# A four-layer graph attention stack on Trainium2: layer 0 with SyncE in program order, x loaded four targets at a time, input copies between the first gathers, and the target bias added by VectorE

## The chip, the core and the metric

The program runs on one core of one Trainium2 chip. The metric is the device time of one execution in microseconds, the median of several runs. The engines are called here as the profile calls them: PE (TensorE), DVE (VectorE), ACT (ScalarE), POOL (GpSimd) and SP (SyncE). SP computes nothing and only issues transfers (DMAs). Transfers are issued from three engines: SP and ACT[...], and POOL[...].[...]

## What is computed

There are 3327 nodes with 256 features, and a symmetric adjacency matrix in which about one entry in a hundred is set, so that a node has some 33 neighbours. Four layers follow each other; each is `x = layernorm(x + attention(x))`. The change touches layer 0 only:

```
g_src = x @ W_src_w.T + W_src_b                      # [n, 256]
g_tgt = x @ W_tgt_w.T + W_tgt_b                      # [n, 256]
score[i, j] = sum_c leaky_relu(g_src[i] + g_tgt[j], 0.2)[c] * a_w[c]
weights = softmax over j of score, only where adj[i, j] != 0
x = layernorm(x + weights @ g_tgt)
```

Because the weights of a row sum to one, `weights @ g_tgt` equals `weights @ (x @ W_tgt_w.T) + W_tgt_b`. The kernel uses this: the table of targets holds the rows without their bias, the bias is put into the source term for the scores, and it is added once to the output.

## The kernel before

Layers 1 to 3 treat the adjacency as dense and are mostly matmuls. Layer 0 (`sparse0`, L269) is sparse: for each node it makes a list of its neighbours, gathers their rows from a table in DRAM, and works on nothing else. The 26 tiles of 128 nodes are split into four sets of 4, 7, 9 and 6 tiles (`SETS`). Within a set nodes are sorted by their number of neighbours, so that a tile needs as many gathers as its largest node: 56 in the first tile of a set, fewer in the later ones (`LEVELS`). Four gathers make a part; there are about 245 parts in all, counted by q.

The work runs in this order.

1. **Setup.** Constants, weights (`w_tgt`, `w_src`), the row `a_row`, the biases in a tile `bias`, and the transposed x in seven banks of 512 nodes (`columns_wide`, L323, issued by ACT at L330). The banks lie in buffers that the gathers use later. `load` (L303) brings pieces of the adjacency, 128 rows by 1024 columns of int32, into three buffers `adj_i`, by SP.
2. **Targets and the neighbour lists of set 0.** A loop over the 26 tiles makes the rows of targets on PE from the banks of x (`targets`), which ACT copies out and POOL stores into `table_d`. Between them run the steps of `neighbours(0)`: ACT converts a piece of the adjacency (`convert`, L524), PE turns it into column numbers (`fill`), and DVE finds the largest eight again and again (`scan` at L560, `sort`), which gives each node's list. `sources` makes the source rows and stores them to `own_d` from ACT. For tiles of later sets it loads its columns of x itself into `xt` (L428, SP, four buffers). At the end DVE ranks the nodes of a set (L659 to L663).
3. **Gathers and scores.** A loop over the parts q runs, at each step: some steps of the later sets' `neighbours`, whatever is due at this step, the gathers of part q + 8 (`LEAD`) on POOL (L756), and the scores of part q on DVE (L776 and L782). After a tile's last part, ACT scales the gathered rows (L829), PE adds them up (L832), DVE adds the input (`add_input`, L852) and POOL scatters the result back (`put_back`, L869). `write_list` (L712) stores the lists of a later set in sorted order, and `read_lists` (L720) reads them back.

Each set has an array `own_d` in DRAM with a row per node: the negated source term, the input row at column 257 (`AT_X`), and the node's own target row at column 513 (`AT_TGT`). `gather_own` (L744) fetches these rows in sorted order. They are put together from four sides: `sources` writes the first part, `keep_inputs` (L384) copies the input from x, DRAM to DRAM, `add_bias` (L389, the transfer at L392) adds `b_tgt` to the input in DRAM with an accumulating transfer on POOL, and a copy on SP brings the target rows from `table_d`.

Who orders the work: within `sparse0` a `manual_schedule` names PE, DVE, ACT and POOL, and these run their instructions in the order of the program. SP isn't named, so the planner of the framework may move its transfers ahead of where the program has them.[...] `at_step(q, ...)` puts a piece of work at step q of the third loop; `between` holds small POOL pieces that are put between two gathers.

In the program the copies for sets 1 to 3 stand after the second loop:

```
            for s in range(1, len(SETS)):
                lo, hi = starts[s] * P, min(n, (starts[s] + SETS[s]) * P)
                keep_inputs(s, nc.sync)
                copy_rows(nc.sync, own_d[s][: hi - lo, AT_TGT:], table_d[1 + lo : 1 + hi, :])
                at_step(4 + 2 * s, between.append, lambda s=s: add_bias(s))
```

In the trace, SP issues the copies of inputs at 9.01 to 26.5 us, the copies of target rows at 83.84, 104.47 and 117.47 us, and POOL the three bias transfers at 201.03, 231.90 and 260.44 us.

Of the kernel before, what the change touches and what calls it, by code (L numbers as in the profile page):

```python
# [8 lines left out]
F32 = mybir.dt.float32  # L9
# [5 lines left out]
ALU = mybir.AluOpType  # L15
# [4 lines left out]
P = 128  # L20
# [4 lines left out]
BIG = 1e30  # L25
# [7 lines left out]
SETS = (4, 7, 9, 6)  # L33
# [10 lines left out]
AT_X = 257  # L44
AT_TGT = 513
# [4 lines left out]
def gat_stack(  # L50
# [29 lines left out]
    nc = tc.nc  # L80
    n, dim = x.shape
# [24 lines left out]
    table_d = dram.tile([n + 1, ROW], F32, name="table_d")  # L106
# [13 lines left out]
    def copy_rows(engine, dst, src):  # L120

        rows = dst.shape[0]
        whole = rows // 16 * 16
        for lo, hi in ((0, whole), (whole, rows)):
            if lo < hi:
                engine.dma_start(dst[lo:hi], src[lo:hi])
# [93 lines left out]
    banks_n = [(lo, min(n, lo + BANK)) for lo in range(0, n, BANK)]  # L220
# [48 lines left out]
    def sparse0(lost):  # L269
        GROUP, TURNS, LEAD, SPREAD = 4, 22, 8, 8  # L270
        starts = [sum(SETS[:s]) for s in range(len(SETS))]
        with ExitStack() as s0:
# [5 lines left out]
                tc.manual_schedule(  # L278
                    engines={
                        mybir.EngineType.PE, mybir.EngineType.DVE, mybir.EngineType.Activation,  # L280
                        mybir.EngineType.Pool,
                    }
                )
            )
# [18 lines left out]
            def load(s, t, p):  # L303
                lo, hi = pieces[p]
                it, pn = starts[s] + t, rows_of(starts[s] + t)
                adj_i = loaded[s, t, p] = io0.tile(
                    [P, PIECE], I32, tag="adj_i", name="adj_i", bufs=3
                )
                copy_rows(nc.sync, adj_i[:pn, : hi - lo], adj[it * P : it * P + pn, lo:hi])

            for p in range(3):
                load(0, 0, p)

            w_tgt = const0.tile([P, kc, ROW], F32, name="w_tgt0")
            nc.scalar.dma_start(w_tgt[:, :, :dim], w_tgt_t.rearrange("(c p) f -> p c f", p=P))
            a_row = const0.tile([P, dim], F32, name="a_row")
# [6 lines left out]
            def columns_wide(b):  # L323
                lo, hi = banks_n[b]
                t = gath.tile(
                    [P, GROUP, ROW], F32, tag=f"g{(TURNS - 1 - b + SHIFT) % TURNS}", name="x_wide"
                )
                t = t.rearrange("p a b -> p (a b)")[:, : kc * BANK]
                t = wide_x[b] = t.rearrange("p (k i) -> p k i", k=kc)
                nc.scalar.dma_start(t[:, :, : hi - lo], x_t_p[:, :, lo:hi])  # L330

            columns_wide(0)
            w_src = const0.tile([P, kc, dim + 1], F32, name="w_src0")
            nc.scalar.dma_start(w_src[:, :, :dim], w_src_t.rearrange("(c p) f -> p c f", p=P))
            bias = const0.tile([1, 2, dim + 1], F32, name="bias0")
            bs_row = bias[:, 0, :]
            nc.scalar.dma_start(bias[:, 0, :dim], b_src[None])
            nc.scalar.dma_start(bias[:, 1, :dim], b_tgt[None])
            for b in range(1, len(banks_n)):
                columns_wide(b)  # L340

            raised = const0.tile([P, P], BF16, name="raised")
            nc.vector.tensor_scalar_mul(raised, ident, float(BASE))
            minus_one = const0.tile([P, P], BF16, name="minus_one")
# [39 lines left out]
            def keep_inputs(s, engine):  # L384

                lo, hi = starts[s] * P, min(n, (starts[s] + SETS[s]) * P)
                copy_rows(engine, own_d[s][: hi - lo, AT_X : AT_X + dim], x[lo:hi, :])

            def add_bias(s):  # L389

                lo, hi = starts[s] * P, min(n, (starts[s] + SETS[s]) * P)
                nc.gpsimd.dma_start(  # L392
                    own_d[s][: hi - lo, AT_X : AT_X + dim],
                    b_tgt[None].to_broadcast([hi - lo, dim]), accum_op=ALU.add,
                )

            keep_inputs(0, nc.gpsimd)
            add_bias(0)

            nc.vector.memset(w_tgt[:, :, dim:], 0.0)  # L400
            nc.vector.memset(w_src[:, :, dim:], 0.0)
            nc.vector.memset(bias[:, :, dim:], BIG)
# [4 lines left out]
            def score_columns():  # L407
                for c in range(kc):
                    t = io0.tile([P, dim], F32, tag="minus", name="dots0")
                    nc.vector.tensor_mul(t, w_tgt[:, c, :dim], a_row)  # L410
                    nc.vector.tensor_reduce(w_tgt[:, c, dim : dim + 1], t, axis=AX.X, op=ALU.add)
                nc.vector.tensor_scalar_mul(w_tgt[:, :, dim], w_tgt[:, :, dim], SLOPE)
                nc.vector.tensor_add(bs_row[:, :dim], bs_row[:, :dim], bias[:, 1, :dim])
                nc.scalar.mul(a_ps[:, :dim], a_row, 1.0 - SLOPE)
                nc.scalar.copy(a_ps[:, dim : dim + 1], ones[:, :1])

# [320 lines left out]
            between = []  # L737
# [114 lines left out]
            def add_input(s, t):  # L852

                entry = held[s, t]
                inv = io0.tile([P, 1], F32, tag="inv0", name="inv0")
                nc.vector.reciprocal(inv, entry["total"])
                y = entry["y"] = io0.tile([P, dim], F32, tag="hs", name="hs")
                nc.vector.scalar_tensor_tensor(
                    y, entry["acc"][:, 0, :], inv, entry["own"][:, AT_X : AT_X + dim],
                    op0=ALU.mult, op1=ALU.add,  # L860
                )
                nc.vector.scalar_tensor_tensor(
                    y, entry["acc"][:, 1, :], inv, y, op0=ALU.mult, op1=ALU.add
                )

            def put_back(s, t):

# [116 lines left out]
            nc.scalar.dma_start(table_d[0:1, :], none)  # L984


            first = neighbours(0)
# [29 lines left out]
            def at_step(q, what, *args):  # L1017
                due.setdefault(q, []).append(lambda: what(*args))
# [40 lines left out]


            ahead, owed, steps = [], {}, 0
            for s in range(1, len(SETS)):
# [827 lines left out]
```

## Time and profile before

| what | value |
|---|---|
| median of 3 runs | 3480.82 us (3480.5 to 3486.92) |
| the profiled execution | 3106.54 us |
| its span, first to last instruction | 3104.8 us |
| mean granted PE clock | 0.866 |
| PE busy | 2339.8 us (75%) |
| DVE busy | 2137.5 us (69%) |
| POOL busy | 1036.3 us (33%) |
| ACT busy | 869.1 us (28%) |
| gathers (L756), POOL | 945, of 949 ns each |
| first gather of layer 0 issued | 126.65 us |
| last scatter of layer 0 issued | 1487.07 us |

The profile describes one execution. Its times count from the first instruction. The page gives the busy time of each engine, the same in 40 equal slices, the groups of instructions that cost most, and what ended the idle time before each group. Other views give the instructions in order of time, the busy time within chosen stretches, and who waited for whom. In a line such as `POOL L756 DMA_INDIRECT g<-table_d,lst` the engine comes first, then the line of the kernel, the operation, and output and inputs by name. An issue of a transfer has a q behind its engine's name (`SPq`, `ACTq`), except on POOL. The time of an issue is not that of the data: the landing is told apart. A bracket at the end of a line holds the idle time before the instruction and what ended it. The DMA share is the mean busy share of the 16 engines.

### The profile page before, as it was taken

The page shows a single profiled execution, that of the slowest core. Times are in us where ns is not written, and L with a number is a line of the kernel's source. Part 1 is how long each engine was busy: PE and PEld are TensorE (multiplying, and loading weights), DVE is VectorE, ACT ScalarE, POOL GpSimd, SP SyncE. Part 2 cuts the span into 40 slices and gives each one's busy share as a digit, 9 for nine tenths or more (in the row PEclk, how much of TensorE's full clock was granted, in tenths as well). Part 3 has the DMA queues.
Part 4 walks back from the last instruction along what each step waited for, and adds up shares of the span by engine and source line. Part 5 has one row for each costly group of instructions (what it writes and reads, how often), then busy time and mean ns, then how long its engine had stood idle before and what let it go on. Part 6 is the DMA issues. An engine that isn't in the chain of part 4 may idle for free.

```text
span 3104.8 us, 45392 instructions
## 1 busy us (share of the span) xinstructions
PE 2339.8 (75%) x16046; PEld 1294.9 (42%) x16046; DVE 2137.5 (69%) x5575; ACT 869.1 (28%) x2426; POOL 1036.3 (33%) x1108
## 2 busy tenths in 40 slices
PE   3554666455454442736799999999999999999997
PEld 2322222222121211313688888884434545444342
DVE  3686988686787535755345532118898899899997
ACT  2233535343343331625234421110110110120110
POOL 1455777777777777776000000000000000000000
PEclk9657767777677776868899999999999999999998
DMA  8687676555654435644677643342212212212211
GB/s 207 195 187 139 171 186 172 141 138 147 146 141 114 114 103 109 147 112 110 207 237 210 196 137 93 102 116 62 66 46 71 68 47 70 66 46 61 56 47 48
DMA packets 183699, 374.90 MB, mean 121 GB/s; under 512 B 34847, under 2 KB 123375, under 8 KB 182440
## 3 DMA queue, kind: packets, MB, share of 16 engines
q0 software_dynamic: 56384, 164.24, 22.0%
q1 hardware_dynamic: 101946, 174.63, 20.2%
q10 hardware_dynamic: 25134, 33.04, 3.1%
q8 instruction: 130, 2.13, 0.3%
q14 instruction: 105, 0.86, 0.1%
HBM read 332.01 MB, written 49.53 MB: 123 GB/s over the span
## 4 chain that ended last, share of the span: by engine, by line
PE 46%; DVE 4%; DMA 1%; issue 1%; ACT 0%; SPq 0%; POOL 0%; POOLq 0%; DVEq 0%; ACTq 0%
PE acc L1545 18%; PE acc L1498 16%; PE acc L1553 9%; PE misc L1344 3%; DVE e L1414 2%; DMA at<-at_d 1%; DMA at_i<-in_adj_t_dram 1%; PE misc L1441 0%; PE misc L1627 0%; PE misc L1588 0%; DVE stats L1705 0%; DVE h L1703 0%; DVE both L1700 0%; DVE h L248 0%; DVE h L1518 0%
## 5 line engine op out<-in xcount | busy, mean ns | idle before, releaser
L756 POOL DMA_INDIRECT g<-table_d,lst x945 | 897.2, 949 | 333.1 <-issue 258.5
L1414 DVE SCALAR_TENSOR_TENSOR e<-rate,feat,at 128x896 f32<-128x896 f32 (+4 forms) x832 | 844.1, 1080 | 80.1 <-PE acc L1553 69.7
L832 PE MATMUL acc<-g,ident 128*128 128x512 f32 x958 | 526.5, 696 | 350.5 <-ACT g L829 321.7
L1545 PE MATMUL acc<-e,feat 128*32 128x384 f32 (+2 forms) x6656 | 688.4, 516 | 4.7 <-DVE e L1414 2.1
L776 DVE TENSOR_TENSOR y<-g,minus_ps 128x1028 f32<-128x1028 f32 (+2 forms) x245 | 289.1, 1180 | 251.8 <-DMA g<-table_d,lst 239.0
L832 PEld LDWEIGHTS acc<-g,ident 128*128 128x128 f32 x958 | 207.1, 225 | 591.8 <-ACT g L829 459.6
L1545 PEld LDWEIGHTS acc<-e,feat 128*32 128x32 f32 x6656 | 259.9, 110 | 342.0 <-issue 229.0
L829 ACT ACTIVATE g<-g,w 128x256 f32<-128x256 f32 x945 | 389.5, 494 | 8.8 <-issue 4.5
L1553 PE MATMUL acc<-e,feat 128*32 128x384 f32 (+3 forms) x3328 | 375.2, 513 | 0.0
L782 DVE SCALAR_TENSOR_TENSOR y<-y,a_ps 128x257 f32<-128x257 f32 x945 | 342.7, 418 | 7.5
L1498 PE MATMUL acc<-feat,e 128*128 128x257 f32 (+2 forms) x1352 | 305.0, 383 | 15.2 <-DMA l3aw<-in_l_w_dram 14.1
L1498 PEld LDWEIGHTS acc<-feat,e 128*128 128x128 f32 (+2 forms) x1352 | 256.3, 192 | 53.0 <-issue 15.1
L242 POOL TENSOR_TENSOR rstds<-rstds,minus_half 128x7 f32<-128x7 f32 (+1 forms) x12 | 19.7, 1644 | 773.0 <-DVE rstds L241 773.0
L534 PE MATMUL v<-code,leads 65*128 65x512 bf16 (+1 forms) x182 | 83.2, 459 | 232.9 <-DVE cand L560 183.5
L1498 PE MATMUL acc<-feat,at 128*128 128x257 bf16 (+2 forms) x2028 | 239.0, 275 | 8.3 <-DMA at<-at_d 8.1
L1498 PEld LDWEIGHTS <-at 128*128 128x128 bf16 (+2 forms) x2028 | 199.1, 99 | 42.9 <-DMA at<-at_d 6.5
L1553 PEld LDWEIGHTS acc<-e,feat 128*32 128x32 f32 (+1 forms) x3328 | 139.8, 110 | 155.4 <-issue 130.3
L560 DVE MAX8 cand<-v 128x8 f32<-128x104 f32 (+2 forms) x858 | 159.1, 260 | 15.5 <-PE v L537 15.5
L1414 DVE SCALAR_TENSOR_TENSOR e<-rate,feat,at_i 128x896 f32<-128x896 f32 (+2 forms) x104 | 111.6, 1081 | 78.9 <-DMA at_i<-in_adj_t_dram 61.2
L1394 POOL DMA_DIRECT2D rate3b_d<-rate_rows x4 | 2.1, 524 | 468.0 <-ACT rate_rows L1393 468.0
L534 PEld LDWEIGHTS <-leads 65*128 65x128 bf16 x182 | 20.4, 112 | 266.7 <-DVE cand L560 219.6
L1431 ACT CAST at<-at_i 128x896 bf16<-128x896 int32 (+2 forms) x104 | 92.0, 885 | 104.3 <-DMA at_i<-in_adj_t_dram 88.3
(205 smaller groups left out, 1776.0 us busy)
## 6 DMA issues: line engine op xcount, KB each, us to landing
adj_i<-in_adj_dram SPq DMA_DIRECT2D x75, 512.0 KB, 4.2
at<-at_d SPq DMA_DIRECT2D x150, 224.0 KB, 2.5
at_i<-in_adj_t_dram SPq DMA_DIRECT2D x50, 448.0 KB, 4.1
g<-table_d,lst POOLq DMA_INDIRECT x945, 2.9
at<-at_d SPq DMA_DIRECT2D x75, 192.0 KB, 2.4
at<-at_d SPq DMA_DIRECT2D x75, 191.8 KB, 2.3
at_d<-at ACTq DMA_DIRECT2D x50, 224.0 KB, 4.3
at_i<-in_adj_t_dram SPq DMA_DIRECT2D x25, 384.0 KB, 3.4
```

The source lines that it names most:

```text
L534: nc.tensor.matmul(v[:, :w], leads[:, b, :], code[:, :w], start=True, stop=False)
L560: nc.vector.max(spread[:, c0 + c, :], view(v[:, :w]))
L756: nc.gpsimd.indirect_dma_start(out=g[:, k - k0, :], out_offset=None, in_=table_d[:, :], in_offset=bass.IndirectOffsetOnAxis(ap=entry["lst" ...
L776: nc.vector.tensor_tensor(y, rows, minus_src[:, None, :].to_broadcast([P, m, dim + 1]), op=ALU.max)
L782: nc.vector.scalar_tensor_tensor(y, y, 1.0, a_ps[:, : dim + 1], op0=ALU.mult, op1=ALU.mult, accum_out=sc)
L829: nc.scalar.activation(rows, rows, AF.Copy, scale=w[:, k : k + 1])
L832: nc.tensor.matmul(dst, ident, rows, start=start, stop=stop)
L1344: nc.tensor.matmul(pacc[:pn, : dim + self.extra], ht[:, k, :pn], self.weight[:, k, :], start=(k == 0), stop=(k == kc - 1),)
L1414: nc.vector.scalar_tensor_tensor(e[:pn, : c1 - c0], self.rate[b][:pn, h_of, : c1 - c0], q, at[:pn, : c1 - c0], op0=ALU.max, op1=ALU.mult,)
L1498: nc.tensor.matmul(accs[s][:pn, : dim + 1], a[:pj, s * P : s * P + pn], f[:pj, : dim + 1], start=(j == 0 and part == 0), stop=(j == nt - 1 ...
L1545: nc.tensor.matmul(accs[x][p][q : q + 32, : hi - lo], f[:pj, at0 : at0 + 32], es[at0 // hd][:pj, lo:hi], start=(j == 0), stop=(j == nt - 1),)
L1553: nc.tensor.matmul(accs[x][pairs][h_of * 32 : (h_of + 1) * 32, : hi - lo], f[:pj, dim + h_of : dim + h_of + 1].to_broadcast([pj, 32]), es[ ...
```

## The change

SP is added to the engines that run in program order within `sparse0`. The banks of x are issued by SP instead of ACT: two before the loop, and the other five in the loop over targets, one every four tiles (at tiles 2, 6, 10, 14 and 18). The tile `bias` is split into a row `bs_row` and a tile `bt_rows`, which holds `b_tgt` in all 128 partitions. The accumulating transfers (`add_bias`) are gone; `add_input` adds `bt_rows` on DVE instead. `keep_inputs(0)` moves from the setup to tile 9 of the target loop. For the sets s = 1, 2, 3 the copy of inputs is put at step 5s of the third loop and the copy of target rows (`keep_targets`) at step 5s + 2; both stay on SP. The table's first row is stored by POOL instead of ACT.

```
-                        mybir.EngineType.Pool,
+                        mybir.EngineType.Pool, mybir.EngineType.SP,
...
-            for p in range(3):
-                load(0, 0, p)
...
-                nc.scalar.dma_start(t[:, :, : hi - lo], x_t_p[:, :, lo:hi])
-
+                nc.sync.dma_start(t[:, :, : hi - lo], x_t_p[:, :, lo:hi])
+
+            load(0, 0, 0)
             columns_wide(0)
+            load(0, 0, 1)
+            load(0, 0, 2)
+            columns_wide(1)
             w_src = const0.tile([P, kc, dim + 1], F32, name="w_src0")
             nc.scalar.dma_start(w_src[:, :, :dim], w_src_t.rearrange("(c p) f -> p c f", p=P))
-            bias = const0.tile([1, 2, dim + 1], F32, name="bias0")
-            bs_row = bias[:, 0, :]
-            nc.scalar.dma_start(bias[:, 0, :dim], b_src[None])
-            nc.scalar.dma_start(bias[:, 1, :dim], b_tgt[None])
-            for b in range(1, len(banks_n)):
-                columns_wide(b)
-
+            bt_rows = const0.tile([P, dim], F32, name="bt_rows")
+            bs_row = const0.tile([1, dim + 1], F32, name="bs_row")
+            nc.scalar.dma_start(bs_row[:, :dim], b_src[None])
+            nc.scalar.dma_start(
+                bt_rows, bass.AP(tensor=b_tgt.tensor, offset=b_tgt.offset, ap=[[0, P], [1, dim]])
+            )
...
-            def add_bias(s):
-
-                lo, hi = starts[s] * P, min(n, (starts[s] + SETS[s]) * P)
-                nc.gpsimd.dma_start(
-                    own_d[s][: hi - lo, AT_X : AT_X + dim],
-                    b_tgt[None].to_broadcast([hi - lo, dim]), accum_op=ALU.add,
-                )
-
-            keep_inputs(0, nc.gpsimd)
-            add_bias(0)
-
...
-                nc.vector.tensor_add(bs_row[:, :dim], bs_row[:, :dim], bias[:, 1, :dim])
+                nc.vector.tensor_add(bs_row[:, :dim], bs_row[:, :dim], bt_rows[:1, :])
...
+                nc.vector.tensor_add(y, y, bt_rows)
...
-            nc.scalar.dma_start(table_d[0:1, :], none)
+            nc.gpsimd.dma_start(table_d[0:1, :], none)
...
             for it in range(nt):
+                if it % 4 == 2 and it // 4 + 2 < len(banks_n):
+                    columns_wide(it // 4 + 2)
+                if it == 9:
+                    keep_inputs(0, nc.gpsimd)
                 row = targets(it)
...
+            def keep_targets(s):
+                lo, hi = starts[s] * P, min(n, (starts[s] + SETS[s]) * P)
+                copy_rows(nc.sync, own_d[s][: hi - lo, AT_TGT:], table_d[1 + lo : 1 + hi, :])
+
             for s in range(1, len(SETS)):
-                lo, hi = starts[s] * P, min(n, (starts[s] + SETS[s]) * P)
-                keep_inputs(s, nc.sync)
-                copy_rows(nc.sync, own_d[s][: hi - lo, AT_TGT:], table_d[1 + lo : 1 + hi, :])
-                at_step(4 + 2 * s, between.append, lambda s=s: add_bias(s))
-
+                at_step(5 * s, keep_inputs, s, nc.sync)
+                at_step(5 * s + 2, keep_targets, s)
```

More of the change, by code (lines that the diff above doesn't have):

```diff
@@ L387, in keep_inputs @@
                 copy_rows(engine, own_d[s][: hi - lo, AT_X : AT_X + dim], x[lo:hi, :])
-            def add_bias(s):
-                lo, hi = starts[s] * P, min(n, (starts[s] + SETS[s]) * P)
-                nc.gpsimd.dma_start(
-                    own_d[s][: hi - lo, AT_X : AT_X + dim],
-                    b_tgt[None].to_broadcast([hi - lo, dim]), accum_op=ALU.add,
-                )
-            keep_inputs(0, nc.gpsimd)
-            add_bias(0)
             nc.vector.memset(w_tgt[:, :, dim:], 0.0)
             nc.vector.memset(w_src[:, :, dim:], 0.0)
-            nc.vector.memset(bias[:, :, dim:], BIG)
+            nc.vector.memset(bs_row[:, dim:], BIG)
             ones = const0.tile([P, P], F32, name="ones")
```

## The prediction

> **What bounds the kernel now.** I read the 40 slices first, then the span in stretches, then each engine's timeline where a stretch looked idle. Two of the slices' lines split the program:
>
> ```profile
> PE   3554666455454442736799999999999999999997
> POOL 1455777777777777776000000000000000000000
> ```
>
> A slice is 3104.8 / 40 = 77.6 us. PE is full only after slice 19, about 1490 us: layers 1 to 3. Layer 0 lies before, and there POOL, at 7 tenths, is as steady as PE is later. The stretches (columns: busy us and count of PE, PEld, DVE, ACT, POOL, then clock, DMA share, GB/s):
>
> ```profile
> 0.00:46.00 46.00, 0.61 (x1) 0.13 (x2) 5.31 (x27) 2.14 (x2) 4.70 (x15) 1.00 0.92 213
> 46.00:125.00 79.00, 59.53 (x205) 37.27 (x205) 52.51 (x265) 31.22 (x86) 16.73 (x31) 0.82 0.72 201
> 125.00:200.00 75.00, 33.75 (x85) 14.13 (x83) 64.42 (x303) 17.08 (x44) 56.58 (x60) 0.55 0.73 185
> 230.00:260.00 30.00, 11.61 (x28) 4.87 (x26) 12.00 (x56) 8.33 (x22) 9.71 (x10) 0.77 0.66 138
> 500.00:600.00 100.00, 54.52 (x128) 22.92 (x126) 66.94 (x274) 44.41 (x115) 76.02 (x81) 0.73 0.58 160
> ```
>
> For 46 us no engine computes while the DMA engines are full. 46 to 125 is the table of targets. From 125 on gathers run at one per 1.25 us (0.95 of work, 0.30 of issue): 81 POOL instructions in 100 us is POOL at its pace. 230 to 260 has 10 where 24 fit. The first hole, on ScalarE:
>
> ```profile
> 5.56 37.88 ACTq L330 DMA_DIRECT2D x_wide<-in_x_t_dram  x6
> 43.53 0.28 ACTq L984 DMA_DIRECT2D table_d<-none  x1
> 43.84 1.28 ACT L524 ACT_TABLE_LOAD   x1 [43.84 <-DMA xt<-in_x_t_dram]
> 45.14 1.06 ACT L524 ACTIVATE adj_b<-adj_i 128x1024 bf16<-128x1024 int32 x1
> ```
>
> Seen is ScalarE held for 37.88 us by six transfers that stand ahead of its first conversion. SyncE had sent the adjacency long before, then the copies of x:
>
> ```profile
> 0.73 1.36 SPq L126 DMA_DIRECT2D adj_i<-in_adj_dram  x3
> 9.01 17.48 SPq L126 DMA_DIRECT2D own_d<-in_x_dram  x4
> ```
>
> The second hole, on POOL:
>
> ```profile
> 201.03 1.38 POOL L392 DMA_DIRECT2D own_d<-in_b_tgt_dram  x1 [0.59 <-DMA g<-table_d,lst]
> ...
> 213.28 0.95 POOL L756 DMA_INDIRECT g<-table_d,lst  x1 [0.30 <-issue]
> 230.19 0.95 POOL L756 DMA_INDIRECT g<-table_d,lst  x1 [15.96 <-DMA own_d<-in_b_tgt_dram]
> ```
>
> After each of the three bias transfers exactly seven gathers go out; the eighth stands until the bias has landed. From this I infer eight transfers in flight per kind of queue. SyncE and ScalarE fit it together: the ninth transfer of the two begins late, at 5.28. All such waits of POOL, and what DVE then lacks (200 to 300 us):
>
> ```profile
> POOL g L756 <- DMA own_d<-in_b_tgt_dram: 42.1, 3, 17.2
> ```
>
> ```profile
> DVE y L776 <- DMA g<-table_d,lst: 36.2, 3, 16.6
> ```
>
> Columns: us in total, times, longest.
>
> [...]
>
> **The change, part by part.**
>
> *The start.* ScalarE now issues five transfers before its table load instead of thirteen; x goes to SyncE, behind the first adjacency piece, two banks of it early. The five slices are about 0.5, 0.5, 0.8, 0.6 and 0.5 us. The last two are ninth and tenth of the two queues and wait for older ones; before, the a_row transfer held SyncE until 9.01. So ScalarE is free near 8.5, loads its table (1.28), and casts at 10.1 instead of 45.14: **35 us**. Ends: only the ninth waits, cast at 7 (38); all first loads slow, cast at 15 (30). What is late next: DVE's setup ends at 7.7; adj_i landed in about 5.6 us; x_wide in 9.8 while in the crowd, and the first is needed 3.3 us after the cast, at 13.4; bt_rows near 12, for L413, which before stood 3.2 us after the cast. All fit within 2 us.
>
> *The body (80 us, from the cast to the first gather).* In DMA work it loses the keep_targets copies: 2815 packets of 67 ns on 16 engines, 11.8 us. It gains five banks of x (256 packets of 96 ns each: 7.7 us at most) and the 512 packets of keep_inputs(0), 68 ns: 2.2. The sum is -2 us at a share of 0.72, so nothing: **0**. Ends: -3 (table writes no longer land beside copies; DVE waited 1.9 for one) and +6 (a bank late: it is sent six targets ahead, six times about 2.5 us, against a landing of 5 to 10). The first row's transfer goes to POOL, about 0.6 us, while POOL waits for rows.
>
> *The bias leaves POOL.* From 199.49 to 280.86 stand 25 gathers, which need 25 x 1.252 = 31.3 us; they took 81.4. The excess of **50.1 us** is three issues (4.2), the 42.1 of waits, and 3.8 around them. POOL's whole account confirms that nothing else is lost: from 125.28 to the last unstalled put_back at 1462.01 are 1336.7 us; 1019 other instructions at 1.2525 need 1276.3; 60 are left, 50 of them these. The bias of set 0 was in the start, and hidden.
>
> *Can DVE follow?* Gathers stand eight parts ahead of scores, and write_list needs DVE's ranks of that step:
>
> ```profile
> 328.53 0.17 DVE L663 CAST ranks_i<-ranks 128x7 uint32<-128x7 f32 x1
> ```
>
> ```profile
> 352.29 0.99 POOL L712 DMA_INDIRECT lists_d<-payload,ranks_i  x1 [0.30 <-issue]
> ```
>
> Take 50.1 from POOL: 302.2. Take its 36.2 us of waiting from DVE: 292.5. POOL still finds the ranks, with 9.7 us to spare. I take all 50.1. If DVE gets 20 us later than this, 10 are lost.
>
> *The copies move to steps 5 to 17 of the gathers.* SyncE issues them; POOL isn't passed. What they add is DMA work: 2815 packets of 68 ns (12.0 us) and 11.8 as above, 23.8 us on 16 engines, over some 80 us whose share is already 0.73. 0.73 x 80 + 23.8 = 82: just full. A gather lands in 2.9 us at the median; POOL stalls only where that passes 8 x 1.25 = 10. A single copy of 1152 packets is 4.9 us of all engines and shares them. **Loss 4 us**; ends 0 and 20. Cover lost, it is 24.
>
> *SyncE in program order.* Its queue is adj_i, xt, the copies, later feats_d. A load of adj_i waits for the conversion three pieces before, as now. xt loses its lead of up to four tiles; it is issued four units before PE needs it, about 8 us, and landed in 6.3 (400 to 1000 us). A late xt holds PE, then DVE, which has 132 us of idle time there. **0**; ends 0 and 6.
>
> *The bias on DVE.* One addition of 128x256 per tile; L410, the same shape, shows 0.42 us[...]. 26 x 0.42 = 11 us, hidden in DVE's idle time; only the last stands in the tail: **0.4**, with nothing else there **0.5**.
>
> **Sum.** 35 + 0 + 50.1 - 4 - 0 - 0.5 = 80.6, say 80. The profiled execution took 3106.5 (span 3104.8 and 1.7 around it): 3026.5. The median of the runs shown is 3480.8, 374 us above; no view shows where. Layers 1 to 3 are PE at a clock of 0.99, so a lower clock there is possible; the two holes are DMA and queue time and I carry the 80 over unscaled: **3400.8**.
>
> **Rivals.** *A: DVE gates POOL.* Copies slow its inputs, the 9.7 us of margin go, POOL waits at write_list. Against: DVE was 86% busy from 125 to 200 with only 1.4 us of waits for PE. For: there is little margin. 35 of the 50 come back as waits: gain 45, 3436. *B: the start hardly moves*, since the first 3 MB still fill the queues and bt_rows lands late; cast at 25, gain 65, 3416. Against: 3 MB at the 312 GB/s of 5 to 10 us is 10 us. *C: slower, by SyncE's order.* Each of 22 tiles of sets 1 to 3 waits for xt. 132 us of DVE idle over some 13 tiles is 10 us each; it costs from there on, and eats the 80 from 14 us per tile. xt landed in 14.1 us from 200 to 290, beside the bias. With 16: 22 x 6 = 132 lost, 3533. For: xt's lead is lost for certain. Against: the crowd that made 14.1 is removed. *D: no change in sum*: half of C, 3480.
>
> **Chances.** Forecast 0.74 (3388 to 3420), A 0.12, B 0.08, C 0.04, D 0.02. Under 0.2% (7 us) this measurement can't tell from none; the runs before spread by 6.4. Faster: 0.94, same 0.02, slower 0.04. The low end is the best bounds, 38 + 3 + 50 = 91: 3390, less 4 for spread. The high end takes in B and reaches A: 3436.
>
> **What would show it.** Right: the first conversion near 10 us, the first gather near 90, no waits for own_d on POOL, about 1286 us from the first gather to the last unstalled put_back, and that one near 1381. Wrong: a first cast after 15 us; gathers waiting for gathers in the first 100 us of them (the copies); POOL waiting at L712 for DVE (A); PE waiting for xt beyond 10 us a tile (C).

## The result, and the profile after

| kernel | executions | median | lowest to highest |
|---|---|---|---|
| before | 12 | 3483.8 us | 3470.5 to 3497.93 |
| after | 12 | 3482.64 us | 3469.11 to 3489.41 |

The ratio is 0.9993, with a 95% interval of 0.9976 to 1.0011: no change. The forecast was 80 us less, or 0.977. The profiled execution of after took 3479.45 us (span 3477.6); the one of before from which the prediction was worked out took 3106.54. In the experiments below all executions of before on one chip took either 3090 to 3103 us (chips 4, 6 and 9) or 3435 to 3495 us (chips 3, 7 and 14), and the twelve of each kernel in the table above are of the second sort. I call them the **3096 executions** and the **3480 executions**.

The slices of the page of after (3477.6 / 40 = 86.9 us each):

```profile
PE   6136445344334433424457999999999999999997
DVE  6267567467365655344463455311588889989998
POOL 2725554654645655665640000000000000000000
```

Layer 0 now ends in slice 21 instead of 19, and POOL, which stood at 7 tenths, stands at 4 to 6. In the span in stretches (columns as before), 500 to 600 is the stretch that showed 81 POOL instructions in the prediction:

```profile
500.00:600.00 100.00, 52.59 (x124) 23.06 (x127) 78.11 (x337) 40.73 (x106) 50.15 (x53) 0.69 0.50 132
```

53 now, while DVE is busier. So POOL no longer sets the pace. Layers 1 to 3 are unchanged: from 1861 to 3477 PE is busy 1565.83 of 1616.00 us at a clock of 0.99, and their 1617 us are those of the execution of 3106 us (1618). What is lost against 3106 is lost in layer 0.

The first hole did close. ScalarE's timeline of after:

```profile
2.88 0.35 ACTq L339 DMA_DIRECT2D bt_rows<-in_b_tgt_dram  x1
4.96 1.28 ACT L513 ACT_TABLE_LOAD   x1 [4.96 <-DMA adj_i<-in_adj_dram]
7.13 1.06 ACT L513 ACTIVATE adj_b<-adj_i 128x1024 bf16<-128x1024 int32 x1 [0.89 <-DVE counts L378]
```

The first conversion begins at 7.13, not 45.14, and the first own gather (`gather_own`, POOL's first indirect transfer) at 86.64. The second hole, POOL behind the bias, is gone too: no wait for own_d is left. In its place POOL's waits from 80 to 1900 us have these rows (us in total, times, longest):

```profile
POOL g L745 <- PE acc L821: 165.0, 21, 76.6
POOL sums_d L859 <- DVE hs L854: 155.3, 18, 23.0
...
POOL lists_d L701 <- DVE ranks_i L652: 44.4, 2, 27.0
```

All three end at DVE (PE's acc at L821 waits 338.0 us in 52 times for ACT's scaling at L818, and ACT's weights at L806 wait 339.0 us in 19 times for DVE's top at L801). The third isn't new, as will be seen: before has 44.3 us of it in a 3480 execution. POOL's timeline has the first of them:

```profile
200.30 0.95 POOL L745 DMA_INDIRECT g<-table_d,lst  x1 [0.30 <-issue]
277.85 0.95 POOL L745 DMA_INDIRECT g<-table_d,lst  x1 [76.60 <-PE acc L821]
```

And DVE's timeline in the gathers ahead of that wait shows why the scores are late:

```profile
106.64 1.20 DVE L765 TENSOR_TENSOR y<-g,minus_ps 128x1028 f32<-128x1028 f32 x1
111.96 0.42 DVE L771 SCALAR_TENSOR_TENSOR y<-y,a_ps 128x257 f32<-128x257 f32 x1 [4.12 <-issue]
...
113.33 0.33 DVE L554 MAX8 cand<-cand 128x8 f32<-128x165 f32 x1
121.11 0.27 DVE L557 MAX8 found<-cand 128x8 f32<-128x107 f32 x1 [7.45 <-remote]
122.52 0.09 DVE L559 MATCH_VALUE_LOAD cand<-found,cand 128x8 f32 x1 [1.13 <-DVE found L557]
...
198.96 0.28 DVE L549 MAX8 cand<-v 128x8 f32<-128x104 f32 x1 [1.81 <-issue]
200.36 0.28 DVE L549 MAX8 cand<-v 128x8 f32<-128x104 f32 x1 [1.12 <-issue]
...
208.21 0.28 DVE L549 MAX8 cand<-v 128x8 f32<-128x104 f32 x1 [1.12 <-issue]
```

L771 at 111.96 needs only the result of L765 just before it, and starts 4.12 us after it. The MAX8 at 121.11 needs only the one at 113.33, and stands 7.45 us. The MAX8s at 198.96, 200.36 and 208.21 carry no wait at all, and stand 1.8, 1.1 and 1.1. I call all of this DVE being **held**. (Delays are those of the instructions themselves; the name behind the arrow, "issue" or "remote" where no releaser was found, is less sure here, for a reason given under "What holds DVE?".) The stretches ahead of POOL's long wait and in it:

```profile
86.64:201.25 114.61, 17.61 (x42) 6.29 (x41) 30.43 (x131) 9.59 (x24) 86.82 (x91) 0.51 0.62 145
201.25:277.85 76.60, 33.14 (x77) 13.86 (x80) 63.42 (x292) 20.19 (x55) 0.00 (x1) 0.52 0.47 134
```

While POOL gathers at its pace DVE gets 131 instructions done in 114.61 us. While POOL stands it gets 292 done in 76.60. It is not free at once: POOL's last gather ended at 201.25, and the last DVE instruction that is held starts at 213.80, 12.6 us later. Nor was it held at once: the first one is that at 111.96, 25 us after the first gather.

### The profile page after: what moved, and what is told of

Its sections match the earlier page's. It is cut to its first block, busy times and chain, and to the rows that moved or that the text cites. A ratio compares the mean times of both kernels' runs of the same rounds, so it can differ in the third digit from the quotient of the medians.

```text
span 3477.6 us, 45402 instructions
## 1 busy us (share of the span) xinstructions
PE 2374.8 (68%) x16025; PEld 1300.2 (37%) x16046; DVE 2160.9 (62%) x5601; ACT 871.6 (25%) x2426; POOL 1031.6 (30%) x1105
## 5 line engine op out<-in xcount | busy, mean ns | idle before, releaser
L821 PE MATMUL acc<-g,ident 128*128 128x512 f32 x958 | 559.4, 729 | 458.0 <-ACT g L818 338.0
L771 DVE SCALAR_TENSOR_TENSOR y<-y,a_ps 128x257 f32<-128x257 f32 x945 | 343.0, 418 | 289.4 <-remote 222.8
L821 PEld LDWEIGHTS acc<-g,ident 128*128 128x128 f32 x958 | 212.8, 233 | 719.8 <-ACT g L818 413.2
L818 ACT ACTIVATE g<-g,w 128x256 f32<-128x256 f32 x945 | 392.2, 495 | 27.7 <-issue 25.4
L765 DVE TENSOR_TENSOR y<-g,minus_ps 128x1028 f32<-128x1028 f32 (+2 forms) x245 | 288.2, 1176 | 38.0 <-issue 26.3
L549 DVE MAX8 cand<-v 128x8 f32<-128x104 f32 (+2 forms) x858 | 171.2, 261 | 154.7 <-issue 107.3
```

Of the source, the lines that this page charges most:

```text
L549: nc.vector.max(spread[:, c0 + c, :], view(v[:, :w]))
L765: nc.vector.tensor_tensor(y, rows, minus_src[:, None, :].to_broadcast([P, m, dim + 1]), op=ALU.max)
L771: nc.vector.scalar_tensor_tensor(y, y, 1.0, a_ps[:, : dim + 1], op0=ALU.mult, op1=ALU.mult, accum_out=sc)
L818: nc.scalar.activation(rows, rows, AF.Copy, scale=w[:, k : k + 1])
L821: nc.tensor.matmul(dst, ident, rows, start=start, stop=stop)
```

## The experiments

From every trace I also took the times of POOL's 1019 indirect transfers, and, for each instruction of DVE that waits for a signal of the instruction just before it, the delay from that one's recorded end.

### In 3096 executions: do the steps hold?

Both kernels as they are, the bias part alone, and after with the copies ahead of the gathers.

> The kernel before, unchanged, profiled a second time. Theory 1 (late signals): the first profile of it, 3106 us, was not what its timed executions do; a second one takes about 3480, layers 1 to 3 keep their 1630 us, layer 0 ends near 1850 instead of 1487, and DVE sits idle for over 200 us behind its own previous instruction while POOL gathers. Rival (clock): layer 0 is as in the first profile and ends near 1487; the 374 us lie in layers 1 to 3 at a lower clock of PE. Timed ratio to before: 1.000 in both.

> The changed kernel, unchanged, profiled a second time. Theory 1: about 3480 again, or, if an execution can escape the late signals, about 3026 (the forecast for the first profile's case). Rival (the change itself makes the late signals, and before has none): 3480 again, always. Timed ratio to before: 1.000.

Measured: 3095.47 us beside 3096.58 (ratio 0.9998, interval 0.9989 to 1.0007), and 3027.32: **0.978** (0.9764 to 0.9796), 69 us faster. The forecast was 80 us, which is 0.974 of 3106. Before's POOL shows the waits of the prediction:

```profile
POOL g L756 <- DMA own_d<-in_b_tgt_dram: 38.9, 3, 16.1
```

After, in its 3096 execution, has these on POOL, among them the counterparts of the three rows above (none is left of that for DVE's ranks):

```profile
POOL g L745 <- issue: 257.7, 843, 1.0
POOL g L745 <- DMA g<-table_d,lst: 25.3, 40, 3.4
...
POOL g L745 <- PE acc L821: 11.6, 38, 0.3
...
POOL sums_d L859 <- DVE hs L854: 0.6, 2, 0.3
```

and its first 114.6 us of gathers:

```profile
83.00:197.60 114.60, 53.81 (x128) 22.84 (x130) 95.40 (x443) 33.22 (x88) 78.25 (x82) 0.55 0.84 224
```

443 instructions of DVE, not 131, beside 82 of POOL. The same program, the same instructions.

> Of the change only the bias: no accumulating transfers, the addition on DVE; the start and the copies as before. If POOL's pace sets the end of layer 0, 50 us less (ratio 0.986). If DVE's delay behind its own signals sets it, POOL's waits for the bias transfers were time in which DVE ran undisturbed, and their removal gives nothing: ratio 0.995 to 1.005.

```
-                nc.gpsimd.dma_start(
-                    own_d[s][: hi - lo, AT_X : AT_X + dim],
-                    b_tgt[None].to_broadcast([hi - lo, dim]), accum_op=ALU.add,
-                )
...
+                nc.vector.tensor_add(y, y, bt_rows)
```

Measured: 3046.47, ratio 0.9849 (0.9831 to 0.9868): 50.1 us. The traces show two parts of it: the first own gather comes 6.0 us earlier (110.19, not 116.19), since set 0's transfer is gone from the start too, and the stretch from there to the third-last scatter is 40.6 us shorter (1291.7, not 1332.3).

> The changed kernel, but with the copies of inputs and targets for sets 1 to 3 issued ahead of the first gather instead of at steps 5 to 17. If the copies among the gathers bring the delays, this is faster than before by 35 us or more (ratio 0.990 or less). If not, within 10 us of the changed kernel.

```
-                at_step(5 * s, keep_inputs, s, nc.sync)
-                at_step(5 * s + 2, keep_targets, s)
+                keep_inputs(s, nc.sync)
+                keep_targets(s)
```

Measured: 3032.72, ratio 0.9793 (0.9777 to 0.981). Against after the first own gather comes 13.4 us later (96.42, not 83.00) and the stretch from it to the third-last scatter is 7.1 us shorter (1295.9, not 1303.0). The place among the gathers is worth 5.4 us net.

> The kernel before once more, on whatever chip comes; one profile is wanted of an execution near 3480. If it takes about 3480: by the theory of late signals, DVE's waits behind its own signals add up to some 500 us in layer 0, they are rare where POOL stands (the three bias transfers), and layer 0 ends near 1850. If it takes about 3095: it only says again that chips differ.

> Of the change the start alone: SyncE in program order, x on SyncE, copies ahead of the first gather, but the bias by accumulating transfers as before. Where executions take 3095: the first gather some 20 us earlier and nothing else, ratio 0.993 to 0.995. Where they take 3480: by the theory of late signals also about 20 us less if only the gathers' stretch is elastic to POOL's waits; 0 if that stretch grows by what the start gives.

```
-                nc.vector.tensor_add(y, y, bt_rows)
...
+                if it == 15:
+                    add_bias(0)
...
+                keep_inputs(s, nc.sync)
+                keep_targets(s)
+                at_step(4 + 2 * s, between.append, lambda s=s: add_bias(s))
```

(This cut is against after: the start is left as it is there.) Measured: before against itself 1.0001 (0.9992 to 1.001); the start alone, with the copies ahead of the gathers and the bias still in transfers, 3072.06: 0.992 (0.9901 to 0.9939), 24 us, with the first own gather at 97.67.

> Of the change only the first line of the diff: SyncE in program order, everything else as before (x still on ScalarE, copies ahead of the gathers, bias by accumulating transfers). Where executions take 3095: the copies of x no longer stand ahead of the banks of x, so part of the start's gain comes from here; an estimate from the start-only run's 24 us is 10 to 20 us less, ratio 0.994 to 0.997; rival C of the prediction (xt late by program order costs more than it saves) says above 1.000. Where they take 3480 by late signals: the profile shows the kernel of before's gathers in that condition, with POOL stalled by DVE rather than DVE by gathers.

```
-                        mybir.EngineType.Pool,
+                        mybir.EngineType.Pool, mybir.EngineType.SP,
```

Measured: 3083.59, 0.9961 (0.9947 to 0.9975): SyncE in program order alone is 12 us faster. Rival C falls for 3096 executions. ScalarE shows why:

```profile
5.49 8.84 ACTq L330 DMA_DIRECT2D x_wide<-in_x_t_dram  x6
...
16.07 1.06 ACT L524 ACTIVATE adj_b<-adj_i 128x1024 bf16<-128x1024 int32 x1
```

The same six transfers that took ScalarE 34.74 us in before's 3096 execution take 8.84 with SyncE's copies of x and its `xt` no longer ahead of them, and the first conversion comes at 16.07, not 41.67. x is still issued by ScalarE.

### What holds DVE?

> The changed kernel with one memset of 128x256 on POOL after each of the 945 gathers, which slows POOL's pace from 1.25 to an estimated 1.6 us (the 128x128 memset took 0.20). Where executions take 3095: POOL sets the end, so 945 x 0.35 = 330 us more, ratio 1.08. Where they take 3480: by the theory of late signals (they come with 15 or more gathers in 20 us, a pace under 1.33) the delays vanish and the time is the pace's own: no slower than the changed kernel, ratio 0.96 to 1.00. If the delays do not depend on POOL's pace: ratio 1.05 or more there too.

```
+            pause = io0.tile([P, dim], F32, tag="pause", name="pause", bufs=1)
...
+                    nc.gpsimd.memset(pause, 0.0)
```

Measured, in 3096 executions: 3213.67, 1.0373 (1.0353 to 1.0394); a gather every 1.445 us, not 1.25. That is less than the 1.08 expected, since the memset took 0.33 us but half of the 0.30 us of issue went under it (0.16 is left). No delay on DVE is over 0.04 us there, so this is only the price of pacing.

> The changed kernel with two tiny copies on SyncE (16 rows of 64 bytes, DRAM to DRAM, nobody reads them) after each of the 945 gathers: some three times as many completion signals per microsecond. If late signals come from the number of signals, DVE's waits behind its own signals appear on any chip (over 0.5 us in more than a third of its waits while POOL runs at its pace) and the time rises by 100 us or more. If they come from POOL's descriptor work itself or from the chip, these waits stay at 0.03 us and the time within 20 us of the changed kernel (the ticks' own DMA work is small).

```
+                    for i in range(2):
+                        tick = ticks[i]
+                        nc.sync.dma_start(tick[ticked[0] % 8], x[:16, :16])
```

Measured, in 3096 executions: 3098.83, 1.0013 (1.0006 to 1.002). 1890 more transfers and their signals cost 71 us against after: DVE waits 58.2 us for PE's v in it, not 7.5, and 37.6 us for ACT's conversions, which I read as SyncE's own loads coming late behind them. That misses the 20 us expected. But DVE's delays stay at 0.02 us, 17 us in all: in a 3096 execution more signals (34 recorded per us of the gathers, not 17) don't hold DVE. In a 3480 execution it wasn't run.

The traces differ in one more thing: how many of their signals they hold. Of some 22,400 signals that instructions and landings in the stretch of the gathers should have left, the trace of after in a 3096 execution has 99.8%, that in a 3480 execution 28% (6260). Ahead of that stretch and behind it nearly all are there (of the signals of landings, 16 for each transfer, the 3480 trace has 1138 of 1152 ahead and all 10,048 behind). It is so in every trace: 28 to 40% in the nine of 3480 executions, over 92% in the others. So in the 3480 traces the name of what ended a wait is often a guess ("remote", "issue", or one that came long before). And it leaves a rival that no run here tests: that the recording of the execution, which loses its signals in the same stretch, is also what holds DVE. Every execution listed in the runs has a span and a granted clock, so each was recorded in some form.

### In 3480 executions: where does the gain go?

The first kernel is before, for its trace; the next three have an equal load on DVE (two more additions of 128x256 behind each weighted score, on idle tiles):

```
                     weighted(y[:, i, :], sc[:, k0 + i : k0 + i + 1])
+                    for _ in range(2):
+                        nc.vector.tensor_add(rest[0], rest[1], rest[1])
```

> The kernel before, for its trace on this chip. If the chip is of the kind that gives about 3480 us, the theory of late signals wants the same sign in it as in the official trace of after: VectorE waiting 1 us and more for its own last instruction while 15 or 16 gathers start in 20 us, some 400 to 500 us of such waits in layer 0, and the last scatter near 1850 us. If it is of the kind that gives about 3096 us, such delays stay at 0.03 us and the last scatter falls near 1473 us.

> The kernel before with two more VectorE additions of 128x256 on idle tiles behind each of the 945 weighted scores of layer 0: 945 x 2 x 0.42 us = 794 us more work for VectorE, so that it and not GpSimd bounds the gathers, as the late signals do on the other kind of chip. VectorE was busy for about 950 of the 1332 us from the first gather of a target's own row to the last regular scatter, so the stretch should come to 1750 to 1790 us and the kernel to 3510 to 3560 us. If GpSimd's pace still decided, it would stay below 3200.

> The same additions in the kernel whose only change is that VectorE adds the bias of the targets. Theory (a stall of GpSimd is worth nothing where VectorE bounds the stretch): 26 x 0.42 = 11 us slower than the kernel before with the same load, within -5 to +15 us. Rival (the 50 us come off whatever bounds the stretch): 50 us faster.

> The same additions in the kernel after. Theory: only the earlier start is left of the gain, against 11 us of additions: 33 us of start less 11, so 15 to 30 us faster than the kernel before with the same load. If the start is also swallowed where VectorE bounds the gathers: within 12 us of it, slower rather than faster. Rival (gains hold): 70 us faster.

Measured, all in 3480 executions (before 3470.64 there): before 3476.39; with the load before 3968.47, bias only 3999.06, after 3967.56 (ratios to the unloaded before 1.1427, 1.1509 and 1.142, each +/- 0.004 to 0.006). The 3510 to 3560 expected for the first was worked out from a 3096 execution, and missed. What counts are the differences: the bias part **lost 31 us** (15 at most were expected), and the rest of the change **gained 31**. So after was level with before (0.9 us faster), where the theory had 15 to 30: it had the sign of the bias's part right and its size too small. The rivals (bias 50, all 70 us faster) fall.

Before is held as after is. These are POOL's waits in before:

```profile
POOL sums_d L869 <- DVE hs L862: 161.1, 19, 23.0
...
POOL lists_d L712 <- DVE ranks_i L663: 44.3, 2, 26.8
...
POOL g L756 <- DMA own_d<-in_b_tgt_dram: 19.6, 2, 11.4
POOL g L756 <- DMA adj_i<-in_adj_dram: 17.8, 1, 17.8
```

There is no single wait of 76.6 us behind PE's acc (the longest has 16.0); the last two rows are the stalls behind the three bias transfers (one put down to the adjacency). Four of its stretches around the first two of these transfers (192.50 and 216.19):

```profile
190.00:202.83 12.83, 0.00 (x0) 0.00 (x0) 3.40 (x13) 1.09 (x4) 10.09 (x10) 0.50 0.88 98
202.83:214.23 11.40, 2.91 (x7) 1.06 (x8) 4.91 (x24) 1.31 (x3) 0.01 (x2) 0.50 0.74 151
214.23:226.60 12.37, 5.19 (x17) 2.65 (x15) 11.51 (x57) 2.67 (x6) 9.22 (x9) 0.64 0.80 94
226.60:244.44 17.84, 9.72 (x22) 4.11 (x23) 16.54 (x80) 5.28 (x13) 0.01 (x1) 0.50 1.04 207
```

From 190 to 202.83 POOL, at its pace since 117.41, goes on, and DVE does 13 instructions in 12.83 us. Then POOL stands from 202.83 to 214.23 behind the first bias. DVE is held for the first 8 us of that and gets 24 done. But in the nine instructions that POOL then does at its pace DVE isn't held (57 in 12.37 us), and in the next stall, from 226.60 on, it does 80 in 17.84; the next instruction that is held starts at 293.4. The stalls that the prediction wanted to remove are the time in which DVE catches up. When the k-th indirect transfer starts, in us:

| k | before, 3480 | bias only, 3480 | after, 3480 | before, 3096 | after, 3096 |
|---|---|---|---|---|---|
| 1 | 117.4 | 110.9 | 86.6 | 116.2 | 83.0 |
| 80 | 250.9 | 210.6 | 186.4 | 253.4 | 194.1 |
| 100 | 293.5 | 317.6 | 287.9 | 285.8 | 219.3 |
| 500 | 980.3 | 1005.8 | 977.5 | 793.5 | 731.1 |
| 1019 | 1854.2 | 1886.6 | 1860.6 | 1473.3 | 1410.7 |

At the 80th, after is ahead by 64.5 us: 30.8 of the start, and the rest stalls that it doesn't have. At the 100th by 5.6: the rest went in the one wait of 76.60 us. From the 100th to the last, before takes 1560.7 us, after 1572.7 and bias only 1569.0: 8 to 12 us more. DVE's added 26 x 0.42 = 11 would fit, but each column is one execution and the three of 3480 ran in different calls, so that isn't shown.

> The kernel before with the bias added by VectorE and nothing else. Where before takes 3096 us it gained 50.1 us. Where before takes about 3475 us: theory (the stalls of GpSimd behind the bias's transfers are pauses in which VectorE's signals come on time; without them it meets the full pace, and it has 11 us more work): 10 to 40 us slower than before, as it was 31 us slower with the load on VectorE. Rival (the gain is only covered, no loss): within 10 us of before or up to 50 us faster.

> The kernel before with the loads of the start ordered as in after, the bias still added by transfers, the copies ahead of the first gather. Where before takes 3096 us it gained 24 us. Where before takes about 3475 us: theory (VectorE starts earlier and is the bound from there on, so the start stays a gain): 15 to 35 us faster than before. Rival (the start is swallowed as well): within 10 us of before.

Edits as above, without a load. Measured, before 3479.69: bias alone 3501.49, ratio **1.0078** (1.0052 to 1.0104), 27 us slower (22 between the medians); start alone 3467.34, **0.9955** (0.9937 to 0.9972), 16 us faster (12 between the medians). As the theory has it, for the start at the small end or just below: here as in the 3096 executions it leaves the copies ahead of the first gather, which cost 13.4 us of start there.

> The kernel after with a memset of 128x256 on GpSimd behind each of the 945 gathers of layer 0, so that 13.8 gathers start in 20 us instead of 16. On a chip on which before takes 3095 us this gave 3214 us. On a chip on which it takes about 3475 us: theory (VectorE's signals come late because GpSimd starts gathers at its full pace): at 12 to 14 gathers in 20 us the traces show a mean delay of 0.2 to 0.6 us in place of 1 to 3.5 us, so most of the 480 us of late signals go, and the kernel takes 3230 to 3400 us: faster than before, although it does more. Rival (the signals are late on that chip whatever GpSimd does, or GpSimd is the bound): 100 to 190 us slower than after, 3580 us or more.

Measured: 3240.42, ratio **0.9316** (0.9291 to 0.9341). The kernel that gives POOL 945 idle memsets more is 7% faster than both kernels, where before takes 3480 us. DVE's waits in it, and those of after:

```profile
DVE y L767 <- DMA g<-table_d,lst: 268.8, 92, 6.5
...
DVE y L773 <- remote: 41.1, 18, 3.2
```

```profile
DVE y L771 <- remote: 222.8, 40, 9.3
DVE cand L549 <- issue: 107.3, 117, 2.0
```

DVE waits for gathers again: POOL is the bound (1297 us of work and 167 of issue in a stretch of 1545). The rival (the holds come whatever POOL does) falls.

> The kernel after with half the memset (128x128) behind each gather: a pace near 1.35 us a gather, between the 1.25 us of after and the 1.445 us of the paced kernel. Where before takes about 3480 us: theory (the delay rises steeply between 14 and 16 gathers in 20 us): some of the late signals come back but less GpSimd time is spent, 3180 to 3330 us. Rival (a threshold close to the full pace): below 3180. Where before takes 3096 us: 3027 + 945 x 0.10 = 3120 us, 3100 to 3135.

The memset is half as wide. Measured, before 3447.82: 3401.25, 0.9848 (0.9816 to 0.9879). Half the pause gives 1.5%, the whole 7%: a smaller gain than the 3180 to 3330 us expected.

> The kernel after with VectorE's steps reordered: the maximum of the next part's rows comes ahead of the weighted scores of this part, so that the first of them waits for a signal that is one part (about 3 us) old, not for the instruction just before it. GpSimd's work and its pace are untouched. Where before takes about 3480 us: that wait cost 290 of the 476 us behind own signals in the trace of after, so theory (the waits for just-issued instructions are the bound): 100 to 250 us faster than before, less than 290 since the rest of the waits then meet a faster pace. Rival (VectorE is slow there for another reason): within 20 us of after. Where before takes 3096 us: 3027 us, as after, within 10 us.

```
+                if q + 1 < len(parts):
+                    rows_max(q + 1)
                 score(q)
```

(A tile's source rows are also laid out one step earlier.) Measured: 3455.76, 1.0024 (1.0012 to 1.0035) of before. The theory expected 100 to 250 us and got nothing: **it falls in this form**. The delays behind own signals fell from 452 to 301 us (148 of them now at L765), but others came up (DVE's waits):

```profile
DVE y L771 <- issue: 142.5, 179, 2.0
DVE y L765 <- remote: 136.5, 26, 9.7
DVE cand L549 <- issue: 101.2, 94, 17.2
```

L771, which no longer waits for the instruction before it, is held all the same. Gaps over 0.5 us ahead of DVE instructions that wait for no signal went from 88 (94.7 us) in after to 181 (193.7 us). So the late signal is one form of the hold and not its cause.

How the hold goes with POOL's pace, as the mean delay behind an own signal:

| indirect transfers begun in the last 20 us | after, 3480 | before, 3480 | paced, 3480 | after, 3096 |
|---|---|---|---|---|
| 4 to 7 | 0.02 | 0.02 | 0.03 | 0.03 (one) |
| 12, 13 | 0.56 | 0.59 | 0.12 | 0.03 |
| 14 | 0.93 | 1.29 | 0.22 | 0.03 |
| 15 | 3.36 | 2.71 | 0.05 (five) | 0.02 |
| 16 | 3.19 | 3.53 | none | 0.02 |

Over the stretch of the gathers the sum is 452 us in after, 470 in before, 122 when paced, 408 at half the pause, and 17 in a 3096 execution. The number in 20 us isn't the whole of it: at 14 the paced kernel has 0.22 us and after 0.93. With the late beginning and end of the hold (in after 25 us behind the first gather, and 12.6 us behind the last one ahead of the long wait) this looks like something that piles up under gathers at full pace and drains after them.

## Why the prediction was wrong

**The step that failed** is the last of the sum: "I carry the 80 over unscaled" from the execution of 3106 us to a median of 3481. It says of the 374 us between them that "no view shows where", and the guess offered was PE's clock in layers 1 to 3. They lie in layer 0, between the first gather and the last scatter: the time from the last scatter to the end is 1618 us in before at 3096 and 1620 at 3480, the stretch of the gathers 1357 and 1737. There DVE, held, is the bound, and POOL's pace, from which the bias step was worked out, isn't. The missing eighth of the time should have stopped the sum: a bound read from one execution says nothing on another that is 12% longer until one knows where that lies. Rival D named the measured 3480 with a chance of 0.02, but by luck: its cause, half of rival C, isn't there: the order alone was 12 us faster where it was measured, at 3096.

- **The start, 35 (30 to 38).** The size is right in both. The first cast moved from 41.67 (45.14 in the execution that the prediction read) to 7.13 us, by 34.5, the first own gather from 116.19 to 83.00 (33.2) at 3096 and from 117.41 to 86.64 (30.8) at 3480, so the body's 0 (at worst 6) holds too. The cause is half right: most of it, 25.6 us at the cast, comes with SyncE's order alone, which the prediction put at 0, with SyncE's early copies no longer among ScalarE's six transfers. The cast came at 7.13, not 10.1, since ScalarE wasn't held. The ninth and tenth transfer of the two queues are SyncE's third adjacency piece and second bank, and those did stand, until 5.35 and 5.72. The eight is the program's own number: in the trace of before the transfers of SyncE and ScalarE (queues q1 and q10, on the page hardware_dynamic) signal on eight semaphores, 100 and 102 to 108, and those of POOL (q0, software_dynamic) on eight others, 109 to 116; the gather at 230.19 in the prediction waits for the semaphore on which the bias of 201.03 signals.
- **The bias leaves POOL, 50.1.** At 3096 the total is the same 50.1, but to the tenth that is luck: 6.0 come at the start, which had been counted as hidden, and 40.6 in the gathers (to the third-last scatter). At 3480 it has the other sign, +27 us: where DVE bounds the gathers a stall of POOL is no loss.
- **Can DVE follow?** Right at 3096, where POOL has no wait for DVE's ranks at write_list. Wrong at 3480, but not at that place: the waits for the ranks are 44.4 us in after and 44.3 in before. New are 76.6 us in one wait for the score of the first tile. This is rival A's mechanism (DVE gates POOL), but not by 9.7 us of margin; it took all 50, and 27 more.
- **The copies, loss 4 (0 to 20).** 7.1 us at 3096 within the gathers; POOL shows 25.3 us of waits for gathers there against 11.6 in before. Moving them was right all the same, by 5.4 us. With the bias's 40.6 less these 7.1, and 3.5 that the order alone costs in the gathers (1335.8 us, not 1332.3, one trace of each), 30 us are left there; 29.3 were measured (1332.3 to 1303.0), and the forecast had 46.
- **SyncE in program order, 0 (0 to 6).** A gain of 12 us by itself at 3096, which lies in the start: the first own gather falls from 116.19 to 102.83. It is part of the start's 35 and isn't to be added to it.
- **The bias on DVE, 0.5.** Hidden at 3096, as far as DVE's 194.6 us of waits for gathers in after tell. At 3480 these waits are 11.5 us, and little is left to cover its 11 us; that they show in full fits, but isn't measured apart.

The start gives -31 us (traces of two calls) and the bias +27 (18 to 36), together -4, beside a measured -2.4 (interval -8 to +4) for the whole change. With the load on DVE, in one call, it is -31.5 and +30.6. The two parts cancel, and that is the result.

**Shown:** that in 3480 executions the hold, and with it the time, follows POOL's pace (paced, half, stalls), that bias and start cancel, and where. **Not shown:** what holds DVE, and why in some executions only. Each chip was seen in one call, so whether it is the chip or the call isn't known either; the execution of 3106 us and the three of 3481 that were given with the kernel before stand in one record without a chip.

Two candidates can be looked at. One is something that a gather takes from DVE while POOL works on it. The MAX8s of L549 at 198.96, 200.36 and 208.21 were held 1.1 to 1.8 us, and in that trace L549 has 107.3 us of waits for which no releaser was found; in after's 3096 execution, with the same gathers beside it, the waits listed for L549 are six, all for PE's v, 7.5 us together. Held instructions that carry no wait start at any point of a gather (52 of the 88 within its first 0.9 us, so not at its end), and in after up to 12.6 us behind POOL's last one. This speaks against something that a gather holds only while it runs; what the two engines might share, no trace here shows. The other is the recording, as said above: signals go missing and DVE is held in the same stretch of the same executions. The pacing could help under both. An execution of before and after that is timed with nothing recorded would tell, and there is none.

## What to carry to other kernels

Ahead of any sum, make the profiled execution account for the time that counts: where they differ by more than the change is to bring, the bound may be another one. A stall on one engine may be what another one catches up in (here 80 instructions of DVE in a stall of 17.84 us, 13 in 12.83 us ahead of the first); before you remove it, look at what the neighbour does in it, in the profile of the execution that counts. And where an engine's instructions start late behind their own kind, try to slow the engine next to it: here 0.33 us of idle work behind each gather gained 7% in 3480 executions and cost 3.7% against before (6% against after) in the others. And count a trace's signals before you trust what it names as the end of a wait.

## What the hardware showed that I had not expected

- One program, six chips, two times for before: 3096 us on three and 3448 to 3480 on three, each steady within a call. The whole difference stands in the gathers (1357 and 1737 us).
- With 16 indirect transfers begun in 20 us DVE gets its own signal 3.2 to 3.5 us late in the mean in 3480 executions (up to 9.7) and 0.02 in the others.
- The hold rises steeply: 0.02 us at 4 to 7 transfers in 20 us, some 0.6 at 12 or 13, about 3 at 15 and 16. It begins 17 to 25 us after the first gather, and in after it lasts 12.6 us beyond the last one ahead of the long wait.
- Instructions that wait for nothing are held too, 88 of them over 0.5 us, 94.7 us in all, 1.13 us at the median.
- For the same program, after, the trace of a 3480 execution has 28% of the signals of this stretch, that of a 3096 execution 99.8%.
